# Last 512 tokens' end of a first layer spread over the turns of the second layer's attention; short rows of the last head pair put last

## The chip, the cores and the metric

The kernel runs on one core of one Trainium2 chip. The metric is device time in microseconds (us). Before the change it is 1535.13 us, the median of three runs (1533.04 to 1536.53). The profiled execution took 1535.0 us; its instructions span 1532.2 us of that, and 2.8 us lie around them.

## The reference

Input is one sequence `x` of 2048 tokens with 128 features, all in float32. Two layers of the same outer form run one after the other:

```
x  = L0_attn_x                                  # 1 x 2048 x 128
xn = layernorm(x)
s  = layernorm(xn + relu_attention(xn) @ w_out + b_out) * gamma + beta    # 16 heads of 8
g  = silu(routed_block(xn))       # 255 chosen tokens: attention, MLP; the others pass through
x  = x + s * g
xn = layernorm(x)
s  = softmax_attention(xn, causal)              # 16 heads of 64, output through W_O, + b_O
g  = silu(h @ w_down), h = silu(xn @ w_gate) * (xn @ w_up)                # hidden size 384
x  = x + s * g
```

The weights of the last feed-forward come as integers and are multiplied by 1/127.

## The kernel before

Tokens lie on the 128 partitions in 16 chunks of 128; four chunks make a block of 512 tokens, and `NQ` is 4 blocks. The order of the instructions on TensorE (PE), ScalarE (ACT) and VectorE (DVE) is the order in which the program calls them, since the whole body runs under a manual schedule; GpSimd (POOL) and the DMA queue of SyncE (SP) are ordered by the framework. [...]

**First layer.** `relu_attention` runs 256 steps (4 query blocks, 4 groups of 4 heads, 16 key chunks). Between the steps a generator `others` is advanced: the routed block, then `gated(qc)` for each query block. `gated` (lines 824 to 874) is the end of the layer for 512 tokens: sums are inverted and sent through DRAM to be widened (`wide<-inverse`, eight DMAs), `on` is multiplied by `wide` on POOL, multiplied by `w_out` on PE (L843), added to `xne` (L847), normalised, gated by `g0`, added to `xin`, normalised again, transposed (L100) and stored in `xn1T` (L191). Its `moments` (L882 to L889) take a square root on ACT (L198) and a Newton step on POOL (L203 to L206). For the first three blocks this is done between steps of the first attention. The last block's sums are only there once the last step has run, so `gated(3)` runs after it.

**Between the layers.** After the steps, `second.opened()` loads the second layer's weights, and `early` (line 1000) runs the feed-forward `ffn(i)` (L1018 to L1030) of blocks 0 to 2 and the first projections of head pair 0: keys 0 and 1, queries 0 and 1, values 0 and 1. `gated(3)` advances by one step after each piece of these. PSUM tiles here come from six one-bank buffers of the first layer. When `gated(3)` has ended, `ffn(3)` runs, and the attention begins.

**Second layer's attention.** `attention` works on 8 head pairs; a pair has 19 turns. A turn `r` holds two slots, each a score tile of two PSUM banks (there are two such tiles). The order of work in a turn is: scores of the turn (L1139), their maxima on DVE (mask L1156, maximum L1157), transposes of the previous turn's exponentials on PE (L1327) with their evictions, two on ACT and the rest on DVE (L1334), the exponentials of this turn on ACT (L1167), products with the values (`z`, L1182), and then what `other` hands out: one of the projections planned in `ahead`, or a step of the end of a finished query block (`divided` L1221/L1224, `output` L1234 to L1246). All PSUM tiles but scores and `z` come from a ring of three one-bank buffers with tag `t`. A score tile is free for the next turn when its exponentials are done.

The turns follow one list for every pair: rows 4 and 5, then 0 and 1, 6 and 7, 2 and 3, then the longer ones, up to rows 14 and 15 over the second half of the keys. Rows 0 to 3 need few keys, so their turns are short.

When the eighth pair's part of a query block is there, `output` adds it to `acc` (L1241), multiplies by the gate `g1` (L1244), adds `x1` (L1245) and stores 256 KB (L1246).

Of the kernel before, what the change touches and what calls it, by code (L numbers as in the profile page):

```python
# [11 lines left out]
F32 = mybir.dt.float32  # L12
F32R = mybir.dt.float32r
BF16 = mybir.dt.bfloat16
I32 = mybir.dt.int32
U32 = mybir.dt.uint32
AF = mybir.ActivationFunctionType
ALU = mybir.AluOpType
# [37 lines left out]
@with_exitstack  # L56
def mixed_layers_kernel(
    ctx: ExitStack,
    tc: tile.TileContext,
    a: dict,  # L60
    out: bass.AP,
):
    nc = tc.nc
    ctx.enter_context(nc.allow_non_contiguous_dma(reason="small weights and rows of sums"))

    const = ctx.enter_context(tc.tile_pool(name="const", bufs=1))
    small = ctx.enter_context(tc.tile_pool(name="small", bufs=4))


    ident = const.tile([P, P], F32, name="ident")  # L70
    make_identity(nc, ident)


    def row_load(name, n, pool):

        t = pool.tile([P, n], F32, name=f"row_{name}")
        nc.sync.dma_start(out=t, in_=a[name].partition_broadcast(P))
        return t


    xin = const.tile([P, NC, D], F32, name="xin")
    xn1T = const.tile([P, S], F32, name="xn1T")
    xsrc = a["x"].rearrange("(c p) d -> p c d", p=P)
    for i in range(NQ):
        nc.sync.dma_start(out=xin[:, 4 * i : 4 * i + 4, :], in_=xsrc[:, 4 * i : 4 * i + 4, :])


    with tc.manual_schedule(
        engines={mybir.EngineType.PE, mybir.EngineType.Activation, mybir.EngineType.DVE}
    ):  # L90
        second = layer1(ctx, tc, a, small, ident, xin, xn1T, row_load, out)
        layer0(ctx, tc, a, small, ident, xin, xn1T, row_load, second)
        second.attention()

# [10 lines left out]
def layer0(ctx, tc, a, small, ident, xin, xn1T, row_load, second):  # L105
    nc = tc.nc

    ends, steps, block = ExitStack(), ExitStack(), ExitStack()
    ps = ends.enter_context(tc.tile_pool(name="l0_ps", bufs=1, space=PSUM))
    dram = ctx.enter_context(tc.tile_pool(name="rb_dram", bufs=2, space=DRAM))  # L110
# [562 lines left out]
def relu_attention(  # L673
# [150 lines left out]
    def gated(qc):  # L824
# [13 lines left out]
        nc.gpsimd.tensor_tensor(on, on, wide, ALU.mult)  # L838
        yield
        yield  # L840
        t = bank([P, 4, D])
        for c4 in range(4):
            nc.tensor.matmul(  # L843
                t[:, c4, :], on[:, c4 * P : (c4 + 1) * P], w_out, start=True, stop=True
            )
        y = end.tile([P, 4, D], F32, tag="y", bufs=1, name="y")
        nc.vector.tensor_tensor(y, t, xne[:, cs, 0:D], ALU.add)  # L847
# [88 lines left out]
    steps.close()  # L936
    second.opened()
    ready.update(range(NQ))
    early = second.early(lambda: bank([P, 512], "s"))
    for _ in range(3):  # L940
        next(early)
    for _ in other:
        next(early, None)
    for _ in early:
        pass
    for _ in second.ffn(NQ - 1):
        pass
# [3 lines left out]
def layer1(ctx, tc, a, small, ident, x1, xn1T, row_load, out):  # L951


# [6 lines left out]
    def ffn_weights(pool, work):  # L960
# [6 lines left out]
        for _ in range(6):  # L967
            yield
        for wi, w in ffn_w.values():
            nc.vector.tensor_scalar(w, wi, 1.0 / 127.0, None, ALU.mult)  # L970
            work.add(d=0.8)
            yield

    def opened():

# [10 lines left out]
        nc.sync.dma_start(out=l1.W_O, in_=a["W_O"].rearrange("n p m -> p n m"))  # L986
        l1.b_o = row_load("b_O", D, lw)

        nc.gpsimd.tensor_scalar(W["W_Q"], W["W_Q"], 0.125, None, ALU.mult)
        nc.gpsimd.tensor_scalar(l1.b_q, l1.b_q, 0.125, None, ALU.mult)  # L990
        l1.g1 = lw.tile([P, NC, D], F32, name="g1")
        l1.acc = lw.tile([P, NC, D], F32, name="acc")

# [5 lines left out]
        )  # L999
        l1.wk = ctx.enter_context(tc.tile_pool(name="l1_w", bufs=2))  # L1000

    def early(bank):

        l1.bank, l1.turning = bank, False
        for i in range(NQ - 1):
            yield from ffn(i)
        for f, i in ((keys, 0), (queries, 0), (keys, 1), (queries, 1), (values, 0), (values, 1)):
            f(0, i)()
            yield


    def ffn(i):
        cols = slice(512 * i, 512 * i + 512)
        hT = l1.f.tile([P, NHB, 512], F32, tag="hT", bufs=2, name="hT")
        for hb in range(NHB):
            hs = slice(hb * P, (hb + 1) * P)
            gate, up = l1.bank(), l1.bank()
            nc.tensor.matmul(gate, ffn_w["w_gate"][1][:, hs], xn1T[:, cols], start=True, stop=True)  # L1018
            nc.tensor.matmul(up, ffn_w["w_up"][1][:, hs], xn1T[:, cols], start=True, stop=True)
            nc.scalar.activation(hT[:, hb, :], gate, AF.Silu)  # L1020
            nc.vector.tensor_tensor(hT[:, hb, :], hT[:, hb, :], up, ALU.mult)
            yield
        t = l1.bank().rearrange("p (c m) -> p c m", m=D)
        for c4 in range(4):
            for hb in range(NHB):
                nc.tensor.matmul(
                    t[:, c4, :], hT[:, hb, c4 * P : (c4 + 1) * P], ffn_w["w_down"][1][:, hb, :],
                    start=(hb == 0), stop=(hb == NHB - 1),
                )
        nc.scalar.activation(l1.g1[:, 4 * i : 4 * i + 4, :], t, AF.Silu)  # L1030
        yield
# [169 lines left out]
    def shares(pr, qc):  # L1201
# [11 lines left out]
        for h in range(n):  # L1213
            w = WIDE[pr, qc, h] = l1.wr.tile([P, 8, 64], F32, tag="wide", name="wide")
            nc.gpsimd.tensor_copy(w, s[:, h, :].unsqueeze(2).to_broadcast([P, 8, 64]))

    def divided(pr, qc, h):
        t = l1.bank().rearrange("p (a b) -> p a b", b=P)
# [4 lines left out]
        def later():  # L1223
            nc.vector.tensor_tensor(ZS[pr, qc, h], ZS[pr, qc, h], t, ALU.mult)  # L1224
            if h:
                nc.vector.tensor_tensor(ZS[pr, qc, 0], ZS[pr, qc, 0], ZS[pr, qc, 1], ALU.add)
# [3 lines left out]
    def output(pr, qc):  # L1230
# [7 lines left out]
        def later():  # L1238
            cs = slice(4 * qc, 4 * qc + 4)
            base = l1.b_o.unsqueeze(1).to_broadcast([P, 4, D]) if pr == 0 else l1.acc[:, cs, :]  # L1240
            nc.vector.tensor_tensor(l1.acc[:, cs, :], t, base, ALU.add)  # L1241
            if pr == NP - 1:
                res = l1.wr.tile([P, 4, D], F32, tag="res", bufs=1, name="res")
                nc.vector.tensor_tensor(res, l1.acc[:, cs, :], l1.g1[:, cs, :], ALU.mult)  # L1244
                nc.vector.tensor_tensor(res, res, x1[:, cs, :], ALU.add)  # L1245
                nc.sync.dma_start(out=out.rearrange("(c p) d -> p c d", p=P)[:, cs, :], in_=res)  # L1246

# [10 lines left out]

    order = []
    for c0, h in (  # L1260
        (4, 0), (0, 0), (6, 0), (2, 0), (8, 0), (8, 1), (10, 0), (10, 1), (12, 0), (14, 0),
        (12, 1), (14, 1),
    ):
        order += four(c0, h)
    per = len(order) // 2
    turns = [
        [[(pr, *row) for row in slot] for slot in order[i : i + 2]]
        for pr in range(NP) for i in range(0, 2 * per, 2)
    ]


    ahead = []
    for pr in range(NP):
        for turn, f, i in (
            (-7, queries, 1), (-6, keys, 0), (-5, keys, 1), (-3, queries, 0), (-2, values, 0),
            (-1, values, 1), (1, queries, 2), (3, keys, 2), (5, values, 2), (7, queries, 3),
            (9, keys, 3), (11, values, 3),
        ):
            ahead.append((pr * per + turn, f, (pr, i)))
    ahead.sort(key=lambda x: x[0])  # L1280
    ahead = ahead[6:]

# [53 lines left out]
    def kept(pr, c0, h, slot):  # L1336
# [6 lines left out]
        if not left[pr, qc]:  # L1343
# [5 lines left out]
            after.append((output, (pr, qc)))  # L1349

    def attention():
        nonlocal todo, n_slots, due, r, waited
        l1.ps = ctx.enter_context(tc.tile_pool(name="l1_ps", bufs=2, space=PSUM))
        l1.wr = ctx.enter_context(tc.tile_pool(name="l1_r", bufs=2, side="right"))
        l1.bank = lambda: l1.ps.tile([P, 4, P], F32, tag="t", bufs=3, name="m").rearrange(
            "p a b -> p (a b)"
        )
        l1.turning = True
        l1.z = l1.ps.tile([P, 2, 2, P], F32, tag="z", bufs=1, name="z")
        while r < len(turns) + 1 or todo or done or after:  # L1360
            slots = turns[r] if r < len(turns) else []
            old = sum(turns[r - 1], []) if 1 <= r < len(turns) + 1 else []
            while done:
                kept(*done.pop(0))
            new = []
            for rows in slots:
                maxima, what = scores(rows)
                maxima()
                new.append((rows, *what))
            evicted(turned(packed(old), [nc.scalar.copy, nc.scalar.copy, nc.vector.tensor_copy]))  # L1370
            for x in new:
                exponentials(*x)
            if after and after[0][0] in (ratios, shares):
                g, args = after.pop(0)
                g(*args)
                waited = r

            if todo:
# [13 lines left out]

            for few in (True, False):
                f = other(r, few)
                if f:
                    f()
            r += 1

    def other(r, small):

        nonlocal waited
        if ahead and ahead[0][0] <= r and not small:
            _, f, args = ahead.pop(0)
        elif after and waited < r and after[0][0] in (divided, output):
            f, args = after.pop(0)
# [63 lines left out]
```

## Time and profile before

| | |
|---|---|
| time, median of three runs | 1535.13 us (1533.04 to 1536.53) |
| profiled execution | 1535.0 us, span 1532.2 us |
| mean granted TensorE clock | 0.989 |
| DVE, ACT, POOL busy | 1109.7 us (72%), 961.6 us (63%), 307.9 us (20%) |
| first layer's attention ends on PE | 522.3 us |
| first score of the second attention | 578.6 us |
| last score of the second attention begins | 1506.9 us |
| last DVE instruction ends | 1528.7 us |
| one pair of heads in between | 117.5 us, of it PE busy 116.4 us |

The page gives busy time of each engine, then 40 slices of the span. A row of the timeline has the start, the time that the merged instructions cover, the engine and line, what is written from what, and in square brackets the idle time ahead of it with its releaser. A row of the chain of waits has the start, the length and what the end of the program waited for at that moment. A row of the table of stretches has the length of the stretch and, for each engine, busy time and number of instructions, then the granted clock. A float32 product on PE shows as two rows each; the fp32r scores and the transposes show as one.

### The profile page before, as it was taken

To read this page: it belongs to the slowest core of one execution; us is meant where nothing else is said; L and a number is where in the kernel's file an instruction comes from. 1 tells how busy PE (TensorE), PEld (TensorE's weight loads), DVE (VectorE), ACT (ScalarE), POOL (GpSimd) and SP (SyncE) were. 2 spreads that over 40 slices of the span, in tenths; PEclk is the share of its full clock that TensorE was granted. 3 is DMA by queue.
4 is the path that set the end of the run, shared out by engine and by line. 5 is a ranking of instruction groups with operands and counts; after the bars stand their busy time and mean duration, and the time that the engine had idled before them with its cause. 6 is when DMAs were issued, how large, how long until landed. Compare 5 with 4: busy or idle time off the path is not lost.

```text
span 1532.2 us, 27033 instructions
## 1 busy us (share of the span) xinstructions
PE 1462.9 (95%) x10374; PEld 886.6 (58%) x10374; DVE 1109.7 (72%) x1985; ACT 961.6 (63%) x2056; POOL 307.9 (20%) x409
## 2 busy tenths in 40 slices
PE   4999999999999968999999999999999999999997
PEld 2223333233222346777777777777777777777775
DVE  5798778877888646667667767767766767767775
ACT  2787778777888635556555655655655655655653
POOL 1000100024000001242242232232231242232210
PEclk9999999999999989999999999999999999999998
DMA  2000100000000210010001001001001001001000
GB/s 64 1 5 3 37 4 4 9 5 27 7 12 9 76 35 15 15 29 15 15 18 25 15 15 28 15 15 29 15 15 28 15 15 29 15 15 24 19 15 14
DMA packets 19681, 29.24 MB, mean 19 GB/s; under 512 B 5024, under 2 KB 13600, under 8 KB 19552
## 3 DMA queue, kind: packets, MB, share of 16 engines
q1 hardware_dynamic: 18864, 26.47, 7.4%
q8 instruction: 81, 1.33, 0.4%
q0 software_dynamic: 256, 0.79, 0.2%
q14 instruction: 48, 0.39, 0.1%
q10 hardware_dynamic: 432, 0.26, 0.1%
HBM read 7.69 MB, written 1.72 MB: 6 GB/s over the span
## 4 chain that ended last, share of the span: by engine, by line
PE 85%; DVE 7%; ACT 6%; issue 1%; DMA 0%; POOL 0%; ACTq 0%; DVEq 0%; POOLq 0%
PE t L1139 17%; PE z L1182 16%; PE t L1327 15%; PE t L801 13%; PE t L785 6%; PE m L1234 2%; PE m L1049 2%; PE m L1084 2%; PE t L695 2%; PE m L1221 2%; PE m L1099 2%; ACT rt L793 2%; ACT pt L1334 1%; DVE rt L795 1%; DVE junk L303 1%
## 5 line engine op out<-in xcount | busy, mean ns | idle before, releaser
L793 ACT ACTIVATE rt<-t 128x512 f32<-128x512 f32 x624 | 329.6, 608 | 73.4 <-PE t L785 72.5
L1157 DVE TENSOR_REDUCE tops<-t 128x1 f32<-128x1024 f32 (+4 forms) x320 | 334.7, 1063 | 53.4 <-PE t L1139 46.4
L1167 ACT ACTIVATE p<-t,tops 128x1024 f32<-128x1024 f32 (+7 forms) x384 | 330.6, 877 | 4.6 <-DVE tops L1157 4.6
L1139 PE MATMUL t<-k,q 128*128 128x512 f32 (+3 forms) x1280 | 319.0, 392 | 8.5 <-ACT p L1167 7.8
L1334 ACT COPY pt<-t 128x512 f32<-128x512 f32 (+2 forms) x320 | 149.2, 523 | 277.5 <-PE t L1327 277.5
L795 DVE TENSOR_SCALAR rt<-t 128x512 f32<-128x512 f32 x400 | 259.2, 684 | 36.7 <-PE t L785 31.9
L1327 PE MATMUL t<-ident,p 128*128 128x128 f32 x2176 | 278.0, 276 | 5.0
L801 PE MATMUL t<-rt,va 128*9 128x512 f32 x2048 | 268.2, 596 | 3.7 <-ACT part L817 3.7
L1182 PE MATMUL z<-pt,v 128*64 128x256 f32 (+1 forms) x2304 | 268.3, 374 | 0.5 <-ACT zs L1341 0.5
L1139 PEld LDWEIGHTS t<-k,q 128*128 128x128 f32 x1280 | 219.2, 189 | 81.3 <-issue 34.4
L1327 PEld LDWEIGHTS t<-ident,p 128*128 128x128 f32 x2176 | 244.4, 141 | 34.8 <-ACT pt L1334 17.2
L1182 PEld LDWEIGHTS z<-pt,v 128*64 128x64 f32 x2304 | 151.9, 136 | 87.3 <-issue 25.2
L1334 DVE COPY pt<-t 128x512 f32<-128x512 f32 (+2 forms) x320 | 180.5, 608 | 1.7 <-PE t L1327 1.7
L785 PEld LDWEIGHTS t<-qT,kT 32*128 32x128 f32 x1024 | 64.6, 181 | 185.2 <-ACT rt L793 112.1
L785 PE MATMUL t<-qT,kT 32*128 32x512 f32 x1024 | 156.9, 497 | 4.9 <-DVE rt L795 2.7
L1156 DVE TENSOR_TENSOR t<-t,mask_q 128x128 f32<-128x128 f32 (+1 forms) x192 | 65.1, 339 | 93.8 <-PE t L1139 85.0
L1072 POOL CAST q<-x 64x512 fp32r<-64x512 f32 x60 | 36.6, 610 | 409.1 <-ACT x L1070 407.3
L1167 ACT ACTIVATION_READ_ACCUMULATOR p<-t,tops 128x1 f32 x384 | 82.4, 215 | 0.0
L1224 DVE TENSOR_TENSOR zs<-zs,m 128x512 f32<-128x512 f32 x48 | 32.8, 688 | 67.1 <-PE m L1221 67.1
L1074 POOL TENSOR_TENSOR k<-x,k 64x512 fp32r<-64x512 f32 x60 | 76.2, 1271 | 4.6
L1074 POOL TENSOR_TENSOR q<-x,q 64x512 fp32r<-64x512 f32 x60 | 76.1, 1269 | 4.6
L1072 POOL CAST k<-x 64x512 fp32r<-64x512 f32 x60 | 36.5, 609 | 173.0 <-ACT x L1070 171.2
(244 smaller groups left out, 1097.1 us busy)
## 6 DMA issues: line engine op xcount, KB each, us to landing
q<-q SPq DMA_DIRECT2D x64, 256.0 KB
xin<-in_x SPq DMA_DIRECT2D x4, 256.0 KB
on<-part SPq DMA_DIRECT2D x64, 16.0 KB
wide<-inverse SPq DMA_DIRECT2D x32, 32.0 KB
out<-res SPq DMA_DIRECT2D x4, 256.0 KB
r_w<-in_w SPq DMA_DIRECT2D x2, 256.0 KB
mdram<-mrows SPq DMA_DIRECT2D x1, 512.0 KB
w_W_K<-in_W_K SPq DMA_DIRECT2D x1, 512.0 KB
```

The lines of the kernel that those rows point to most:

```text
L785: nc.tensor.matmul(t, kT[rows, g, kb * P : (kb + 1) * P], qTs[qc, g][rows, :], start=True, stop=True,)
L793: nc.scalar.activation(rt, t, AF.Relu, scale=scale)
L795: nc.vector.tensor_scalar(rt, t, scale, 0.0, ALU.mult, ALU.max)
L801: nc.tensor.matmul(acc[32 * j : 32 * j + HD0 + 1, :], va[:, kb, 4 * g + j, :], r[j], start=(kb == 0), stop=(kb == NC - 1),)
L1072: nc.gpsimd.tensor_copy(high, x[half(e), :])
L1074: nc.gpsimd.tensor_tensor(low, x[half(e), :], high, ALU.subtract)
L1139: nc.tensor.matmul(flat[:, lo + x : lo + y], q[:, part, c4 * P : (c4 + 1) * P], k[:, x:y], start=(part == 0), stop=(part == 1),)
L1157: nc.vector.tensor_reduce(M[pr, c // 4][:, h, c % 4, es], x, AX.X, ALU.max, negate=True)
L1167: nc.scalar.activation(p[:, lo : lo + n], flat[:, lo : lo + n], AF.Exp, bias=M[pr, c // 4][:, h, c % 4, e : e + 1], accum_out=Z[pr, c // 4 ...
L1182: nc.tensor.matmul(l1.z[half(e), slot, lo:2, :], V[pr, h][:, kb, half(e)], pts[e][:, kb, lo:2, :], start=(kb == 0), stop=(kb >= n0 - 1), s ...
L1327: nc.tensor.transpose(t[:, k + b, :], x[lo + b], ident)
L1334: copy(dst, t)
```

## The change

The end of the first layer for the last 512 tokens stops after its product with `w_out` and the addition to `xne`, which writes into `second.y`, the last four chunks of `acc`. The rest of it, and the whole feed-forward of that block, is cut into 12 pieces by `tail` that run at the ends of turns of pair 0. To keep what the pieces need, POOL copies the gate `g0` of that block and the three feed-forward weights. The square root becomes an integer estimate on DVE with four Newton steps on POOL.

The PSUM pool of the second layer opens right after the first layer's steps, so the feed-forwards of blocks 0 to 2 and the first projections also use its ring of three banks. Their order becomes: `ffn(0)`, then queries 1, keys 0 and keys 1 mixed with the parts of `ffn(1)`, the scores and maxima of turn 0, `ffn(2)` with queries 0 in it. Values 0 and 1 move into turn 0, queries 2 into turn 1. The gate of block 2 is kept raw, and its Silu is taken together with three other tiles in the piece of the third gate product.

In the last pair the rows 2, 3, 0 and 1 go to the end. `acc` is multiplied by the gate and added to `x1` on POOL after the seventh pair, so that the last `output` needs two DVE operations rather than three. The last query block is divided, added and stored in two halves. Once the turns are over, all of `ratios` and `shares`, and up to four steps of `other`, are taken in each round.

```diff
@@ relu_attention, gated
-        yield
-        yield
-        t = bank([P, 4, D])
+        for _ in range(2 if qc < NQ - 1 else 6):
+            yield
+        if qc < NQ - 1:
+            t = bank([P, 4, D])
+        else:
+            t = second.bank().rearrange("p (a b) -> p a b", b=D)
...
+        if qc == NQ - 1:
+            nc.vector.tensor_tensor(second.y, t, xne[:, cs, 0:D], ALU.add)
+            return
@@ relu_attention, after the steps
     steps.close()
-    second.opened()
+    second.opened(g0)
     ready.update(range(NQ))
-    early = second.early(lambda: bank([P, 512], "s"))
+    early = second.early()
     for _ in range(3):
         next(early)
     for _ in other:
-        next(early, None)
+        next(early)
     for _ in early:
         pass
-    for _ in second.ffn(NQ - 1):
-        pass
     ends.close()
@@ layer1, opened
+        end = slice(NC - 4, NC)
+        l1.y, l1.gate = l1.acc[:, end, :], l1.g1[:, end, :]
+        nc.gpsimd.tensor_copy(l1.gate, g0[:, end, :])
+        for n, (w,) in list(ffn_w.items()):
+            kept = lw.tile(list(w.shape), F32, name=f"f_{n}_last")
+            nc.gpsimd.tensor_copy(kept, w)
+            ffn_w[n] = w, kept
...
+        l1.ps = ctx.enter_context(tc.tile_pool(name="l1_ps", bufs=2, space=PSUM))
+        l1.bank = lambda: l1.ps.tile([P, 4, P], F32, tag="t", bufs=3, name="m").rearrange(
+            "p a b -> p (a b)"
+        )
+        l1.turns, l1.turning = attention(), False
@@ layer1, early
-        for i in range(NQ - 1):
-            yield from ffn(i)
-        for f, i in ((keys, 0), (queries, 0), (keys, 1), (queries, 1), (values, 0), (values, 1)):
+        yield from ffn(0)
+        hidden = ffn(1)
+        for f, i in ((queries, 1), (keys, 0), (keys, 1)):
             f(0, i)()
             yield
+            next(hidden)
+            yield
+        yield from hidden
+        next(l1.turns)
+        yield
+        hidden = ffn(NQ - 2)
+        next(hidden)
+        yield
+        queries(0, 0)()
+        yield
+        yield from hidden
@@ layer1, new
+    def moments(x):
...
+        for i in range(4):
+            nc.vector.bn_stats(st[:, i, :], x[:, i, :])
+            nc.vector.bn_aggr(mv[:, i, :], st[:, i, :])
+        nc.vector.tensor_scalar(v, mv[:, :, 1], 1e-5, None, ALU.add)
+        yi = y.bitcast(I32)
+        nc.vector.tensor_scalar(yi, v.bitcast(I32), 1, None, ALU.arith_shift_right)
+        nc.vector.tensor_scalar(yi, yi, -1.0, float(0x5F3759DF), ALU.mult, ALU.add)
+        for i in range(4):
+            nc.gpsimd.tensor_tensor(t, y, y, ALU.mult)
+            nc.gpsimd.tensor_tensor(t, t, v, ALU.mult)
+            nc.gpsimd.tensor_scalar(t, t, -0.5, 1.5, ALU.mult, ALU.add)
+            nc.gpsimd.tensor_tensor(r if i == 3 else y, y, t, ALU.mult)
+        return mv, r
+
+    def tail():
...
+        def first():
+            got.append(moments(y))
+        def gated():
+            mv, r = got.pop()
+            for c in range(4):
+                nc.vector.scalar_tensor_tensor(
+                    y[:, c, :], y[:, c, :], mv[:, c, 0:1], g[:, c, :], ALU.subtract, ALU.mult
+                )
+            for c in range(4):
+                nc.vector.scalar_tensor_tensor(
+                    x[:, c, :], y[:, c, :], r[:, c : c + 1], x[:, c, :], ALU.mult, ALU.add
+                )
+        def second():
+            got.append(moments(x))
+        def normal():
...
+        def turn():
+            t = l1.bank().rearrange("p (a b) -> p a b", b=P)
+            for c in range(4):
+                nc.tensor.transpose(t[:, c, :], y[:, c, :], ident)
+            return lambda: nc.scalar.copy(xn1T[:, cols], t.rearrange("p a b -> p (a b)"))
...
+        def raw(hb, t):
+            nc.scalar.copy(hs[hb], t)
+            if hb == NHB - 1:
+                for h in hs + [l1.g1[:, NC - 8 : NC - 4, :]]:
+                    nc.scalar.activation(h, h, AF.Silu)
+        def times(hb, t):
+            nc.vector.tensor_tensor(hs[hb], hs[hb], t, ALU.mult)
+        def down():
...
+            return lambda: nc.scalar.activation(g, t, AF.Silu)
+        out = [(f, (), False) for f in (first, gated, second, normal)] + [(turn, (), True)]
+        for n, later in (("w_gate", raw), ("w_up", times)):
+            out += [(hidden, (n, hb, later), True) for hb in range(NHB)]
+        return out + [(down, (), True)]
@@ layer1, output
+            if pr < NP - 1:
+                base = l1.b_o.unsqueeze(1).to_broadcast([P, 4, D]) if pr == 0 else acc
+                nc.vector.tensor_tensor(acc, t, base, ALU.add)
+                if pr == NP - 2:
+                    nc.gpsimd.tensor_tensor(acc, acc, g1, ALU.mult)
+                    nc.gpsimd.tensor_tensor(acc, acc, x1[:, cs, :], ALU.add)
+                return
...
+            for x in pieces(pr, qc):
+                nc.vector.tensor_tensor(res[:, x, :], t[:, x, :], g1[:, x, :], ALU.mult)
+                nc.vector.tensor_tensor(res[:, x, :], res[:, x, :], acc[:, x, :], ALU.add)
+                nc.sync.dma_start(out=dst[:, x, :], in_=res[:, x, :])
@@ layer1, the order of the turns
+        if pr == NP - 1:
+            order = [x for x in order if x not in ((0, 0), (2, 0))] + [(2, 0), (0, 0)]
...
+                (0, queries, 2), (2, keys, 2), (4, values, 2), (5, queries, 3), (7, keys, 3),
+                (9, values, 3), (11, queries, 0),
@@ layer1, attention, end of a turn
-            for few in (True, False):
-                f = other(r, few)
+            for few in (r > 2, False, True, True)[: 4 if ending else 2]:
+                f = other(r, few, ending)
+                if not f and few and pieces and pieces[0][2]:
+                    g, args, _ = pieces.pop(0)
+                    f = g(*args)
                 if f:
                     f()
+            if pieces and not pieces[0][2]:
+                g, args, _ = pieces.pop(0)
+                g(*args)
             r += 1
```

## The prediction

> **What bounds the kernel now.** I read the page first, then the granted clock and busy times in short stretches round the change of layers, then the timeline there and at the end, then the chain of waits.
>
> ```profile
> PE 1462.9 (95%) x10374; PEld 886.6 (58%) x10374; DVE 1109.7 (72%) x1985; ACT 961.6 (63%) x2056; POOL 307.9 (20%) x409
> ...
> PE 85%; DVE 7%; ACT 6%; issue 1%; DMA 0%; POOL 0%; ACTq 0%; DVEq 0%; POOLq 0%
> ```
>
> PE bounds the program as a whole: a pair of heads takes 117.5 us, 116.4 of them with PE busy. So the change can gain only where PE stands still, and PE work moved into the turns costs its full time. The table of stretches shows where it stands still:
>
> ```profile
> 552.00:556.00 4.00, 1.80 (x17) 1.61 (x15) 3.81 (x9) 3.91 (x7) 0.23 (x1) 1.00 0.17 37
> 556.00:560.00 4.00, 0.00 (x0) 0.00 (x0) 3.74 (x9) 0.62 (x1) 0.79 (x4) 0.62 0.70 175
> 560.00:564.00 4.00, 0.00 (x0) 0.00 (x0) 3.29 (x14) 0.16 (x1) 0.22 (x1) 0.50 0.15 50
> ...
> 580.00:582.00 2.00, 0.23 (x2) 0.03 (x1) 1.90 (x3) 1.12 (x1) 0.00 (x0) 1.00 0.00 0
> 582.00:584.00 2.00, 0.89 (x5) 0.68 (x5) 0.00 (x0) 1.93 (x5) 0.00 (x0) 1.00 0.00 0
> 584.00:586.00 2.00, 2.00 (x9) 1.80 (x9) 1.53 (x4) 0.00 (x0) 0.00 (x0) 0.56 0.00 0
> ```
>
> PE's busy time is the first figure after the length. DVE and ACT work through the end of the first layer while PE has nothing: 12.0 us idle in one piece. After it PE runs at half clock, and each of turns 0 to 2 waits again for maximum and exponential. From 540 to 600 PE is idle 18.5 us. The end is a chain of single steps:
>
> ```profile
> 1515.90 3.48 PE z L1182 x32
> ...
> 1520.97 0.62 POOL wide L1215
> ...
> 1522.34 1.30 DVE zs L1224 x2
> ...
> 1524.49 2.06 PE m L1234 x8
> ...
> 1528.03 0.69 DVE res L1245
> ```
>
> Last score 1506.91, last DVE end 1528.72, end 1532.2.
>
> **Up to turn 0: PE 523.1 to 559.6.** PE work, from the rows: three feed-forwards of six products at 0.86 and 24 half-products at 0.11 (7.8 each, 23.3), four projections at 0.86 (3.4), scores of turn 0 (1.66), `w_out` (0.9): 29.3. The start waits for the eviction of the old accumulator, on which the first product now depends (523.08 rather than 522.29). What is added in waits:
> - Queries 1 comes right after `ffn(0)`, about 531.7, but POOL ends scaling `w_W_Q` at 533.02 (its row starts 530.24, when the weights land). Wait 1.5. The four POOL copies ahead of it (0.61 and three of about 0.45) end before 530 and cost nothing.
> - Three banks in place of six. A projection holds its bank for two ACT rows (1.38) and the last of two DVE rows (0.75 each): about 2.5. Between it and the next use of that bank PE has 1.72 of work. Wait 0.8 for keys 0, keys 1, the `down` of `ffn(1)` and `w_out`, 3.2; bounds 0 (a bank free in time) and 1.2 each.
> - The last factor of each `down` waits for DVE: 0.4 to 0.9, about 2.1 for three.
>
> The sum is 36.2; with handovers I take 559.6. On SP the two DMAs of queries 1 now stand ahead of the eight `wide` loads. Those wait for `inverse` until 536.75 anyway, about when queries 1 is split; a delay of 1 us is covered, as `w_out`'s product stands at about 553 and `on` was ready at 544.7.
>
> **Turns 0 to 4: 559.6 to 586.4.** A turn's first score needs the exponential of the turn before, that needs the maximum, and the maximum stands on DVE behind the piece put at the end of the turn. Pieces on DVE: `first` and `second` 2.3 each (four pairs of 0.28 and 0.18 with gaps, three small ones), `gated` 2.3, `normal` 1.4. Each `moments` also puts 16 POOL steps of 0.28 ahead of the piece that follows: 4.5.
> - S1: raw copy, table load 1.28, exponential 1.0 after 559.6: 562.6.
> - S2: `values` added to 562.5, `first` to 564.8, maximum 1.15, exponential 1.0: 567.0.
> - S3: POOL to 569.4, `gated` to 570.6, short rows' maxima 2.1, four short exponentials 1.8: 574.6.
> - S4: maximum 574.1, evictions 1.0, `second` to 577.4, then PE's own work: 580.7.
> - S5: POOL to 582.0, `normal` 583.4, maximum 1.6, exponential 1.35: 586.4.
>
> Before, S5 is at 605.65, so 19.2 are won there. PE's own work in this stretch is about 20 of 26.8 us, so the pieces bound it, not PE. POOL's split of queries 2 comes 4 us later than it would; it is not needed until turn 5, where before had 18 us.
>
> Here **the clock rule** bears. The Trainium skill ("TensorE: Matmul & The Clock Gate", What's actually happening) gives half clock after about 3.4 us idle. The row is sharper: after the gap from 580.24 to 583.11, only 2.9 us, the clock is 0.56. By the rule one gap (before S3) would count, 1.7 us of half speed; by rows like those of 580 to 600 (mean 0.83) 20 us of work loses up to 4, half of it beside other waits. I take 1.5; bounds 0 and 3.5.
>
> **Left over for later turns.** Of `ffn(3)` the six products and `down` still run on PE: 5.2 + 2.6 = 7.8, full price. The transposes are in S5 already.
>
> **Silu among exponentials.** Two switches to Silu and back are put into turns 7 and 15. The trace:
>
> ```profile
> 552.34 1.38 ACT L1063 ACTIVATE k<-t,b_k 64x512 fp32r<-64x512 f32 x2
> ...
> 553.73 1.28 ACT L198 ACT_TABLE_LOAD   x1
> ...
> 555.02 0.21 ACT L198 ACTIVATE y<-ln_v 128x4 f32<-128x4 f32 x1
> ```
>
> The load starts when the row before ends, and the next starts when it ends: 1.28 in all. The skill ("ScalarE: Activation LUTs", What ACT_TABLE_LOAD costs) counts another 1.38 of drain per switch, and its Rules for kernel authors say to do all of one set before switching, which speaks against this change. In turn 7 ACT gets a copy 0.6, a load 1.28, four Silu 2.4, where its gap up to the next eviction is 2.05 (1494.86 to 1496.91): PE's fourth transposition bank comes 2.2 late. Then the load of Exp puts the exponentials 1.28 back, of which 0.7 shows. Turn 15: 0.5. Together 3.4 by the row, 8.9 by the rule (four drains more). I take 3.4; bounds 1 and 8.9. The loads taken out (Sqrt, Silu) lie in the stretch that is gone.
>
> Front: 19.2 − 1.5 − 7.8 − 3.4 = **6.5 won**.
>
> **The end.** Moving rows 0 to 3 takes the wait of turn 2 out of the last pair (before it PE waits 4.0 for DVE and ACT, with 1.2 of work in it: 2.8) and 0.7 of small evictions. After the last scores PE now has 15.7 of work (transposes 3.1, `z` 6.9, the rest 5.7) against 13.6, so those scores come 2.1 earlier too: 5.6 in all. But what follows is longer. From their start: maxima 5.0; evictions, two exponentials of 0.9 and four of 0.44 to 7.2; last bank 8.4; `z` of rows 14 and 15 waits behind that in PE's order, 11.9; its copy, the ratios, POOL 14.2, transposes and DVE 17.1, product 18.4, two DVE steps 19.9. The reciprocal of rows 0 to 3 stands behind these on DVE, so its chain runs on its own: 20.1, POOL 20.8, PE 21.4, DVE 22.2, product 23.4, last half 25.0, store 3.0 (before: 3.5 for 256 KB). That is 28.0 against 25.3: 2.7 lost. Net **2.9 won**; bounds −2.5 (the earlier scores not had) and +6 (the two chains overlap). The second store costs 0.4 of issue, inside the 3.0. POOL's eight steps of 1.27 in pair 6 lie beside POOL idle 73% of a pair; uncovered they would delay queries 2 by 2.5, four turns before it is due.
>
> **Sum** against the profiled execution: 1535.0 − 6.5 − 2.9 = 1525.6. The median of the runs, 1535.13, is the same within 0.02%. About 0.2% (3 us) is what a measurement of this kernel can tell from no change.
>
> **Rivals.**
> 1. *Pieces hide, PE bounds the first turns.* For: DVE was only 70% busy. If the pieces delay no maximum, S5 comes 7 earlier, Silu costs 1: 6.5 + 7 + 2.4 + 2.9 = 18.8, 1516. Against: the order on DVE puts each piece ahead of the next maximum. 0.20.
> 2. *Switches at the rule's price, or an end without gain.* 5.5 or 2.9 to 5.4 dearer: 1529 to 1531, taken as 1531. 0.20.
> 3. *Slower: the ring of three.* From turn 4 to 15 eight pieces each take a bank that ACT or DVE must empty before the transposes go on. The chain of waits has such a stop in before: 0.59 for an eviction with 0.45 of transposes behind it. If each piece costs one turn's stop plus an exponential (0.6 + 1.1 = 1.7), 13.6 are lost: 1539. From 1.2 per piece it eats the whole gain. Against: evictions of full banks in before mostly hide beside `z`. 0.09.
> 4. *It doesn't do what it says*: if waits up to S1 eat the lead (S5 near 596 rather than 586), 1535. 0.05.
>
> The forecast has 0.46, its own range 1520 to 1529.
>
> **Numbers.** Range 1513 to 1534: below, rival 1 with an end at +6; above, the bounds of Silu and of the end together. Faster 0.87, same 0.04, slower 0.09.
>
> **What would show it.** No idle PE over 5 us between 523 and 590; S1 at 562 to 563, S5 at 584 to 589; in turn 7 loads of 1.28 with an idle PE of 2 to 3; `w_W_Q` holding PE near 531.7; at the end a reciprocal on DVE behind the last but one result, and 27 to 29 us from the last scores to the end. It is wrong if pair 0 after turn 5 loses more than 4 beyond 7.8, or later pairs differ from 117.5.

## The result, and the profile after

The changed kernel takes 1529.55 us (median of six runs, 1529.15 to 1530.31), the kernel before 1535.93 in the same comparison (six runs, 1533.04 to 1536.9). The ratio is 0.9961, with a 95% interval of 0.9948 to 0.9974: faster, by 2.6 to 5.2 thousandths. The profiled execution took 1529.64 us with a span of 1527.5, against 1535.0 and 1532.2 before.

First the page of the changed kernel, its busy times and the shares of the chain of waits. Nothing in them answers the question of where the gain came from; PE is the bound as before, with the same number of instructions.

```profile
PE 1462.7 (96%) x10374; PEld 884.6 (58%) x10374; DVE 1110.9 (73%) x1988; ACT 965.7 (63%) x2060; POOL 324.5 (21%) x443
...
PE 84%; DVE 7%; ACT 6%; issue 2%; DMA 0%; POOL 0%; SPq 0%; ACTq 0%; POOLq 0%; DVEq 0%
```

The table of stretches of the changed kernel, over the same microseconds as before, shows it (columns as before: length, then busy time of PE, weight loads, DVE, ACT and POOL with the number of instructions, granted clock, DMA):

```profile
552.00:556.00 4.00, 3.58 (x15) 2.00 (x14) 2.79 (x4) 1.74 (x4) 0.00 (x0) 1.00 0.32 66
556.00:560.00 4.00, 3.59 (x29) 3.17 (x29) 0.69 (x1) 0.39 (x2) 0.00 (x0) 1.00 0.19 66
560.00:564.00 4.00, 2.91 (x20) 2.46 (x20) 2.92 (x11) 3.45 (x6) 0.00 (x0) 1.00 0.00 0
564.00:568.00 4.00, 3.86 (x26) 2.89 (x25) 3.86 (x11) 2.74 (x7) 2.44 (x13) 1.00 0.02 4
568.00:572.00 4.00, 2.34 (x15) 1.75 (x15) 3.82 (x7) 1.12 (x3) 3.54 (x8) 1.00 0.00 2
572.00:576.00 4.00, 0.00 (x0) 0.00 (x0) 3.86 (x7) 0.92 (x5) 0.84 (x1) 0.85 0.60 131
576.00:580.00 4.00, 3.15 (x8) 2.57 (x9) 3.72 (x16) 1.78 (x6) 0.32 (x2) 0.50 0.00 0
```

From 552 to 564, where PE was busy 1.8 of 12 us, it is now busy 10.1. But from 572 to 576 it has nothing at all, DVE is full, POOL is full in the row ahead, and half clock follows. The prediction reckoned with a pause before turn 3 (it put those scores at 574.6 and counted one gap there for the clock), but not with one of 6.4 us.

To see where the rest is, the span is cut at four moments that every version has: the first product of the feed-forward, the scores of turn 5, the first scores of pair 1, the last scores. Each figure is a difference of two start times on PE's timeline (the last one to the end of the span). Predicted are the prediction's own terms (64.8 is 586.4 - 523.1 plus 1.5 for the clock; 100.5 is 89.3 + 7.8 + 3.4).

| stretch, us | before | predicted | after |
|---|---|---|---|
| wait ahead of the first product | 0 | 0.8 | 0.8 |
| first product to turn 5 | 83.4 | 64.8 | 66.5 |
| turn 5 to pair 1 | 89.3 | 100.5 | 99.0 |
| pair 1 to the last scores | 811.9 | 806.3 | 809.6 |
| last scores to the end | 25.3 | 28.0 | 28.9 |

The front (the first three rows) won 6.35 us, with 6.5 predicted. The end (the last two) was to win 2.9 and **lost 1.3**. The sum is 5.1; the first layer ended 0.4 later in this execution, which makes the 4.7 of the span, and 0.7 less lay outside the span. So the gain was 5.4 us between the profiled executions and 6.4 between the medians, where 9.4 was predicted.

The end, in the chain of waits of the changed kernel (start, length, what the end waited for):

```profile
1498.71 2.05 PE t L1269 x12
...
1506.68 4.28 PE z L1312 x40
...
1512.48 0.62 POOL wide L1345
...
1515.16 0.70 DVE zs L1364
...
1516.00 1.14 PE m L1372 x8
...
1517.96 0.69 DVE res L1391
1518.65 0.12 DVE sums L1339
...
1519.59 0.67 PE m L1357 x4
...
1520.83 2.09 PE m L1372 x8
...
1524.19 0.42 DVE res L1391
```

The division of rows 12 to 15 (POOL at 1512.48, its factors on DVE to 1515.86), its product at 1516.00, then all of it again for rows 0 to 3, whose reciprocal (L1339) starts when the result of the others is ready. The last product takes 2.09 where the one at 1516.00 takes 1.14: PE had stood still for 2.46 us before the transposes of 1519.59 and for 0.58 after them, and its granted clock was 0.55 from 1520 to 1523.

### The profile page after: what moved, and what is told of

Same layout as the page of the kernel before. It is cut to its first block, busy times and chain, and to the rows that moved or that the text cites. A ratio compares the mean times of both kernels' runs of the same rounds, so it can differ in the third digit from the quotient of the medians.

```text
span 1527.5 us, 27075 instructions
## 1 busy us (share of the span) xinstructions
PE 1462.7 (96%) x10374; PEld 884.6 (58%) x10374; DVE 1110.9 (73%) x1988; ACT 965.7 (63%) x2060; POOL 324.5 (21%) x443
## 4 chain that ended last, share of the span: by engine, by line
PE 84%; DVE 7%; ACT 6%; issue 2%; DMA 0%; POOL 0%; SPq 0%; ACTq 0%; POOLq 0%; DVEq 0%
PE t L1269 17%; PE z L1312 16%; PE t L1481 14%; PE t L802 13%; PE t L786 6%; PE m L1372 2%; PE m L1179 2%; PE m L1214 2%; PE t L696 2%; PE m L1229 2%; PE m L1357 2%; ACT rt L794 2%; ACT pt L1488 1%; DVE rt L796 1%; DVE junk L304 1%
## 5 line engine op out<-in xcount | busy, mean ns | idle before, releaser
L1312 PEld LDWEIGHTS z<-pt,v 128*64 128x64 f32 x2304 | 151.8, 136 | 87.1 <-issue 24.9
L1362 DVE TENSOR_TENSOR zs<-zs,m 128x512 f32<-128x512 f32 (+1 forms) x49 | 32.8, 675 | 63.6 <-PE m L1357 63.4
L802 PEld LDWEIGHTS t<-rt,va 128*9 128x9 f32 x2048 | 30.7, 88 | 68.5 <-issue 60.0
```

Of the source, the lines that this page charges most:

```text
L802: nc.tensor.matmul(acc[32 * j : 32 * j + HD0 + 1, :], va[:, kb, 4 * g + j, :], r[j], start=(kb == 0), stop=(kb == NC - 1),)
L1312: nc.tensor.matmul(l1.z[half(e), slot, lo:2, :], V[pr, h][:, kb, half(e)], pts[e][:, kb, lo:2, :], start=(kb == 0), stop=(kb >= n0 - 1), s ...
```

## Experiments

The experiments are compared with runs of the kernel before on the same chip beside them; its medians there lay between 1535.2 and 1535.8. The table has the stretches as above. In runs with the same code, turn 5 to pair 1 agrees within 0.1, pair 1 to the last scores within 0.4, the last stretch within 0.6 (but for e9), so a microsecond is read more safely here, though from one profiled execution of each run, than from the times, whose intervals are 3 to 5 us wide. The first stretch is less steady: before and e3 have the same front and differ by 2.9, since half clock lasted longer in e3 (from 568 to 572 the granted clock was 0.68 in before and 0.50 in e3).

| run | time, us | ratio to before, 95% interval | product to turn 5 | turn 5 to pair 1 | pair 1 to last scores | last scores to end |
|---|---|---|---|---|---|---|
| changed kernel | 1529.55 | 0.9961 (0.9948 to 0.9974) | 66.5 | 99.05 | 809.6 | 28.9 |
| e1_old_order | 1526.00 | 0.9938 (0.9925 to 0.9952) | 66.2 | 99.05 | 811.8 | 24.5 |
| e2_front_only | 1527.92 | 0.9946 (0.9933 to 0.9960) | 66.5 | 99.03 | 811.9 | 25.5 |
| e3_end_only | 1537.29 | 1.0008 (0.9999 to 1.0016) | 86.3 | 89.35 | 809.4 | 29.3 |
| e4_queries2_early | 1529.07 | 0.9953 (0.9940 to 0.9967) | 68.3 | 99.02 | 809.6 | 29.3 |
| e5_early_shares | 1523.81 | 0.9924 (0.9911 to 0.9938) | 66.5 | 99.01 | 809.3 | 23.3 |
| e6_early_shares_old_order | 1524.15 | 0.9927 (0.9913 to 0.9941) | 66.5 | 99.02 | 811.9 | 21.4 |
| e7_no_silu | 1527.85 | 0.9950 (0.9936 to 0.9963) | 66.5 | 97.33 | 809.7 | 29.3 |
| e8_queries2_early_pool | 1527.84 | 0.9950 (0.9936 to 0.9964) | 64.9 | 99.02 | 809.7 | 29.4 |
| e9_both | 1522.67 | 0.9914 (0.9900 to 0.9928) | 64.9 | 99.04 | 809.6 | 24.9 |
| e10_no_pieces | 1522.49 | 0.9913 (0.9897 to 0.9928) | 59.5 | 99.02 | 809.7 | 28.9 |

### The two halves of the change apart: e2 and e3

e2 has the front of the changed kernel and the whole end of before; e3 the other way round. e2 against the changed kernel, cut to its core:

```diff
+            base = l1.b_o.unsqueeze(1).to_broadcast([P, 4, D]) if pr == 0 else l1.acc[:, cs, :]
+            nc.vector.tensor_tensor(l1.acc[:, cs, :], t, base, ALU.add)
+            if pr == NP - 1:
+                res = l1.wr.tile([P, 4, D], F32, tag="res", bufs=1, name="res")
...
-        if pr == NP - 1:
-            order = [x for x in order if x not in ((0, 0), (2, 0))] + [(2, 0), (0, 0)]
...
-        if pr == NP - 1:
-            plan = [
...
```

> The changed kernel with the whole end of before (order, three DVE steps, one store per block). My theory: the front alone wins 5.9 us, so 1529.6 beside 1535.5, and first scores of pair 1 come 5.9 earlier than before; that is the whole gain of the change, so no difference from the changed kernel beyond 1 us. Rival, the prediction's sum: 6.5 of 9.4 won, and the changed kernel 2.9 faster than this.

> Before with the new end alone (last pair's order, gate on POOL, halves, several steps a round). My theory: 1.0 to 1.3 us slower than before, the last scores 2.6 earlier and 28.9 us from them to the end. Rival, the prediction: 2.9 us faster than before.

The front alone takes 1527.92 us. In the stretches it is the changed kernel up to pair 1 and the kernel before after it. The end alone takes 1537.29, a ratio of 1.0008 (0.9999 to 1.0016): no gain, and on the stretches (809.4 + 29.3 against 811.9 + 25.3) 1.5 us slower. The rival, 2.9 us faster, is out. By the stretches the new end costs 1.0 us in the changed kernel and 1.5 in the kernel before; the times alone tell neither from nothing.

### The order of the last pair: e1

```diff
-        if (pr, qc) == (NP - 1, 0):
+        if (pr, qc) == (NP - 1, NQ - 1):
             return [slice(0, 2), slice(2, 4)]
...
-        if pr == NP - 1:
-            order = [x for x in order if x not in ((0, 0), (2, 0))] + [(2, 0), (0, 0)]
-        if pr == NP - 1:
-            plan = [
...
```

> The changed kernel with the last pair's turns and projections back in the order of the other pairs; the gate on POOL and the two halves of the last output stay (now for rows 12 to 15). My theory now: the new order brought the last scores only 2.6 us forward and made the stretch from them to the end 3.6 longer. So here the last scores come 2.6 later than in the changed kernel, and from them to the end it takes 25.3 - 0.7 (one DVE step fewer) - 0.5 (half a store) = 24.1 instead of 28.9: 2.2 us faster than the changed kernel, about 1527.4. Rival, the prediction's sum: last scores 5.6 later, so 0.8 slower than the changed kernel, about 1530.4.

The last scores come 2.25 later and the rest is 4.3 shorter: 2.1 won, as the theory said, and the time is 1526.00. So the other parts of the new end (one DVE step fewer, two halves) are good for 0.8 (837.2 from pair 1 to the end before, 836.4 here), where 1.2 was expected, and the order loses 2.1.

Why the last scores moved so little is seen in the kernel before. Its PE rows in the last pair, from the scores of turn 2 to those of turn 3:

```profile
1410.28 2.30 PE L1139 MATMUL t<-k,q 128*128 128x128 f32 x12
...
1412.41 1.71 PE L1327 MATMUL t<-ident,p 128*128 128x128 f32 x11
...
1414.05 1.30 PE L1182 MATMUL z<-pt,v 128*64 128x256 f32 x12
...
1415.82 2.08 PE L1139 MATMUL t<-k,q 128*128 128x512 f32 x8 [0.46 <-ACT p L1167]
```

The 4 us from 1411.8 to 1415.8, in which DVE and ACT make maxima and exponentials, hold 3.0 us of PE's own work, the transposes and the products with the values, and the last 0.6 of the scores ahead of them, not 1.2. PE waits 0.46, and 1.1 us in all between the first and the last scores of this pair (0.45 in the changed kernel). From the first scores of pair 1 to the last scores PE is busy 804.1 us before and 802.3 in the changed kernel: of the 2.3, 1.8 are PE work that moved behind the last scores, and about 0.6 are waits.

### The hole before turn 3: e4 and e8

DVE and POOL on the changed kernel's timeline, from the gated piece on, and the scores of turn 3:

```profile
567.61 1.21 DVE L1081 SCALAR_TENSOR_TENSOR acc<-acc,mv,g 128x128 f32<-128x128 f32 x4
...
568.90 1.27 POOL L1202 CAST q<-x 64x512 fp32r<-64x512 f32 x2
569.00 3.99 DVE L1085 SCALAR_TENSOR_TENSOR xin<-acc,inv,xin 128x128 f32<-128x128 f32 x4 [0.18 <-POOL inv L1062]
...
570.25 2.59 POOL L1204 TENSOR_TENSOR q<-x,q 64x512 fp32r<-64x512 f32 x2
...
576.85 3.57 PE L1269 MATMUL t<-k,q 128*128 128x512 f32 x8 [6.38 <-ACT p L1297]
```

Four steps of one shape take 1.21 at line 1081 and 3.99 at line 1085. Taken singly, the first of the slow ones runs 569.00 to 569.65 and the third 570.24 to 571.66. POOL splits queries 2 at that time: two casts of 0.61, then two subtractions of 1.27 (their length everywhere), the first of them from 570.25 to about 571.5. DVE's third step, which has two tensor inputs in SBUF like POOL's subtraction, ends 0.1 us after it.

e4 takes the split away from there: the projection of queries 2 goes ahead of the rest of `ffn(2)`, before the turns. e8 does the same but splits on POOL rather than on ACT and DVE. The edit of e8 (in e4 `queries(0, 2)()` stands in the place of the four lines):

```diff
         queries(0, 0)()
         yield
+        later = queries(0, 2)
+        l1.turning = True
+        later()
+        l1.turning = False
+        yield
...
-    ahead = ahead[4:]
+    ahead = [x for x in ahead[4:] if x[1:] != (queries, (0, 2))]
```

> The changed kernel with queries 2 of pair 0 projected before the down product of ffn(2) rather than in turn 1, so that POOL's split of it (1.27 for each half) no longer lies beside the gated piece on DVE. My theory: DVE's four steps at line 1085, which took 0.65 to 1.42 us each beside that split, fall to about 0.36 each like the four at line 1081 just before; that frees 2.6 us on DVE, and PE has one product (0.9) more ahead of turn 0's values. Scores of turn 3 come 1.5 earlier, the time is 1 to 1.7 us less than the changed kernel's. Rival: the steps are long by themselves (three operands in SBUF, or the half clock's stretch), they stay at 1.0 each and the time is 0.9 longer.

> As e4, but with the split of queries 2 done on POOL in the way of the later turns (one copy on ACT), while POOL is idle, so that its bank is held for 0.7 rather than 4 us. In e4 the gated piece's four steps fell to 0.35 each (2.7 us won on DVE) and 3.7 us were lost before turn 1, because ACT and DVE did that split and PE waited 1.38 and 0.47 for its bank. Theory: turn 1 comes only about 1.0 later than in the changed kernel, turn 3 1.7 earlier, the first scores of pair 1 1.5 earlier. Rival: the time won on DVE is taken up again by another wait before turn 5 and pair 1 comes no earlier.

In e4 the four steps fell to 0.35 each, so the mechanism holds. Its time did not: turn 1 came 4.2 later after the first product (43.4 instead of 39.2 us), because there ACT and DVE split queries 2 and PE waited 1.38 and 0.47 for the banks; then it ran at half clock (0.57 from 556 to 560, a gate product 1.91 instead of 1.02). 1.0 to 1.7 less was expected, and there is no difference. In e8 turn 1 is only 0.7 later, and the steps take this (its DVE timeline):

```profile
567.83 1.13 DVE L1086 SCALAR_TENSOR_TENSOR acc<-acc,mv,g 128x128 f32<-128x128 f32 x4
569.38 1.14 DVE L1090 SCALAR_TENSOR_TENSOR xin<-acc,inv,xin 128x128 f32<-128x128 f32 x4 [0.42 <-POOL inv L1067]
```

and turn 5 comes 1.6 earlier. The time is 1527.84, 1.7 less than the changed kernel, which the times alone could not tell from nothing. From these stretches I estimate that the contention cost turn 5 about 2.3 us: 1.6, and the 0.7 that moving the projection costs. A pause of 3.68 before turn 3 is left in e8, and half clock after it (0.50 from 576 to 580).

### What the pieces on DVE cost: e10

e10 leaves out the two norms, the gate and the addition to `x` for the last 512 tokens.

```diff
-        out = [(f, (), False) for f in (first, gated, second, normal)] + [(turn, (), True)]
+        out = 4 * [(lambda: None, (), False)] + [(turn, (), True)]
```

> The changed kernel with the four DVE pieces at the ends of turns 0 to 3 (the two norms, the gate and the addition to x for the last 512 tokens) left out, with nothing in their place; the pieces on PE stay where they are. It prices what those four pieces cost the first turns. Prediction: DVE bounds turns 0 to 4 and the pieces cost about 7 us there, plus the 2.6 that the split on POOL adds; then the fifth turn's scores come 57 to 59.5 us after the first feed-forward product, instead of 66.5. Rival 1 of the prediction (the pieces hide beside PE's work): they come at 63 to 66, the 2.6 of the split at most.

Turn 5 comes at 59.5, 7.0 earlier, at the edge of what the prediction's reading expects and far from the rival. The stretches of e10 lack the hole, and with it the half clock:

```profile
568.00:572.00 4.00, 2.21 (x15) 1.61 (x14) 3.78 (x7) 2.61 (x12) 3.61 (x4) 1.00 0.04 8
572.00:576.00 4.00, 3.83 (x23) 2.98 (x25) 3.02 (x6) 2.38 (x7) 0.13 (x1) 1.00 0.57 125
576.00:580.00 4.00, 4.00 (x24) 2.63 (x23) 1.82 (x5) 2.34 (x5) 0.75 (x2) 1.00 0.00 0
```

If the two add up, about 2.3 of the 7.0 are the split on POOL (the estimate from e8) and 4.7 the pieces with the half clock that they bring; how much of the 4.7 is the clock, no run shows. The pieces do bound the first turns.

### Silu among the exponentials: e7

ACT and PE in turn 7 of the changed kernel:

```profile
610.01 1.28 ACT L1117 ACT_TABLE_LOAD   x1
...
611.30 1.15 ACT L1117 ACTIVATE acc<-acc 128x512 f32<-128x512 f32 x2
...
614.12 1.18 PE L1481 MATMUL t<-ident,p 128*128 128x128 f32 x6 [1.17 <-ACT x L1200]
...
615.32 1.28 ACT L1297 ACT_TABLE_LOAD   x1
...
616.62 1.11 ACT L1297 ACTIVATE p<-t,tops 128x1024 f32<-128x1024 f32 x1
```

Each load is followed by its activation 1.29 to 1.30 after its start, so there is no drain on top; PE waits 1.17.

```diff
-                    nc.scalar.activation(h, h, AF.Silu)
+                    nc.scalar.copy(h, h)
...
-            return lambda: nc.scalar.activation(g, t, AF.Silu)
+            return lambda: nc.scalar.copy(g, t)
```

> The changed kernel with the Silu of the last blocks' feed-forward (the four tiles in turn 7 and the gate in turn 15) left out, copies in their place, so that no table is loaded among the exponentials. My theory, from the trace: PE stood 1.2 us for it in turn 7 and nothing in turn 15, so the stretch from turn 5 to the first scores of pair 1 gets 1.2 to 1.5 shorter (97.6 instead of 99.05). The prediction's price was 3.4 (95.6), the price with the drain that the Trainium skill counts 8.9 (90.1).

The stretch is 97.33, so the switches cost 1.7 us, all of them in turn 7: half of the prediction's 3.4, a little over my later 1.2 to 1.5, and a fifth of the 8.9 estimated by the rule of the Trainium skill ("ScalarE: Activation LUTs", What ACT_TABLE_LOAD costs).

### Dividing before the end: e5, e6 and e9

The sum of the exponentials is known when the last exponential is done; the program asked for the reciprocal only after the products with the values. In e5 `ratios` and `shares` of the last pair's end blocks are called right after their exponentials, and their factors are transposed behind `z`. The edit does one thing more: what `other` hands out once the turns are over (`f`, the DVE steps behind the output products) is held back in `held` until the last product has been asked for. e6 is that on e1. e9 is e5 with e8.

```diff
+    def shared(slots):
+        for pr, c, h, e in sum(slots, []):
+            if pr == NP - 1 and c // 4 in final:
+                rows_of[c // 4] -= 1
+                if not rows_of[c // 4]:
+                    if halves(c // 4) == 2:
+                        ratios(pr, c // 4)
+                    shares(pr, c // 4)
...
             for x in new:
                 exponentials(*x)
+            shared(slots)
...
+                        if not keys_of[c // 4]:
+                            todo += [(widened, (pr, c // 4, i)) for i in range(halves(c // 4))]
                     todo.append((lambda *x: done.append(x), (pr, c // 2 * 2, h, slot)))
...
-                if f:
+                if f and ending:
+                    held.append(f)
+                elif f:
                     f()
```

> The changed kernel, with the new order; the reciprocals of the last pair's first and last query blocks (ratios, shares, the widening on POOL) are issued as soon as their exponentials are, not after their z products, and the widened factors are transposed on PE right behind z. My theory: the new order loses at the end because two divisions run one after the other behind z, 28.9 us from the last scores to the end; with the divisions ahead of z the second block's chain lies beside the first's: the last DVE step comes 6.4 earlier, so 22.5 from the last scores to the end and about 6 us less than the changed kernel, near 1523. Rival: the end is bound by z and the small exponentials (PE in order), not by the divisions; then it gains under 2.

> The same early divisions on the run with the old order of the last pair (e1), for rows 12 to 15. One division instead of two was behind z there, so it gains less: z's end to the multiplication was about 3.0, now 1.2, so 1.8 less than e1, 22.7 from the last scores to the end. If e5 is faster than this by 1 to 3 us, the new order is worth its 2.6 only with early divisions; if this is faster, the new order is not worth it in either form.

> e5 (early divisions, new order) and e8 (queries 2 early, split on POOL) together. The two lie in stretches that don't touch, so their gains should add: 1.6 in the front (first scores of pair 1 163.9 us after the first feed-forward product instead of 165.5) and 5.5 at the end (23.3 instead of 28.9 from the last scores to the end, with pair 1 to the last scores at 809.3): about 1522.3, 7 less than the changed kernel and 13 less than before. Rival: the earlier start is eaten somewhere between, and it stays at e5's 1523.8.

The end of e5 on its timeline:

```profile
1505.33 0.20 DVE L1339 RECIPROCAL sums<-sums 128x8 f32<-128x8 f32 x1 [0.86 <-ACT p L1297]
...
1512.43 0.69 DVE L1362 TENSOR_TENSOR zs<-zs,m 128x512 f32<-128x512 f32 x1 [1.18 <-ACT zs L1495]
...
1514.39 1.95 PE L1372 MATMUL m<-w_W_O,zs 128*128 128x128 f32 x16
...
1518.13 0.43 DVE L1391 TENSOR_TENSOR res<-res,acc 128x256 f32<-128x256 f32 x1
```

The reciprocal of rows 0 to 3 is at 1505.33 instead of 1518.57, and both output products run as one row of 16. The last scores are 23.3 from the end, 5.6 less (6.4 expected), and the time is 1523.81. I estimate that about 0.9 of the 5.6 is the clock: 16 output products take 1.95 here, where the last 8 of the changed kernel took 2.09 alone. What of the rest is due to the early reciprocals and what to holding back the last DVE steps, no run separates. From pair 1 to the end the four forms take, by the stretches:

| | division behind z | division ahead of z |
|---|---|---|
| rows 12 to 15 last | 836.4 (e1) | 833.3 (e6) |
| rows 0 to 3 last | 838.5 (changed kernel) | 832.6 (e5) |

So the new order turns from a loss of 2.1 into a gain of 0.7 once the divisions lie ahead. The 0.7 is below what the times can tell (1523.81 and 1524.15), and the 1 to 3 us expected were not seen; that part stays open. e6 also won more than the 1.8 expected: 3.1. Most of the excess is clock again: its widening and output products behind `z` take 1.09 and 1.49, those of e1 1.67 and 2.05.

e9 takes 1522.67 us, a ratio of 0.9914 (0.9900 to 0.9928) to before, faster than both kernels. It is 1.1 less than e5, where 1.5 was expected; its front has the 1.6. In its profiled execution the last `z` (32 products) took 5.15 instead of 3.46 in e5, with a granted clock of 0.61 from 1504 to 1508, so the end shows 24.9 there.

## Why the prediction came out as it did

The direction was right and the mechanism of the front was right, but 1525.6 was 4 us too low, and nearly all of it is one step: **the end**. The 1529.55 lies just above the 1520 to 1529 that I gave my own forecast, and in the 1529 to 1531 of the second rival.

- **"Moving rows 0 to 3 takes the wait of turn 2 out of the last pair … 2.8 … and 0.7 of small evictions"** is the step that failed. The last scores came 2.3 earlier, not 5.6. I counted a stretch in which the chain of waits lay on DVE and ACT as idle time of PE; PE's own rows show 0.46 of waiting there. Of the 5.6 only the 2.1 of moved work is nearly confirmed (1.8); waits gave 0.6.
- **The tail**: 28.0 predicted, 28.9 measured. Step by step it fits (last bank 8.4 and 8.0, reciprocal of rows 0 to 3 done at 20.1 and 20.1 after the last scores); the last product took 2.09 rather than 1.14, at half clock, and that is the 0.9. I had allowed 1.2 for it, though the row of before that I showed has 2.06 for the same product. Net −1.3 in place of +2.9, inside the bounds given (−2.5), whose lower one was "the earlier scores not had".
- **Up to turn 0**: 559.6 predicted, 559.61 in the trace. That it fits so closely is luck: PE waited 4.2 us rather than 6.8 (`w_W_Q` 1.19 for 1.5, the banks about 1.25 for 3.2, the factors of `down` 1.76 for 2.1), and its own work took 31.9 rather than 29.3. The terms as written also add to 36.1, not 36.2.
- **Turns 0 to 4**: turn 1 562.6 and 562.65, turn 2 567.0 and 566.58, as reckoned; turn 3 2.3 late, turn 5 3.6 late (1.5 of it priced as clock). What was missing is the split of queries 2 on POOL beside the gated piece: I priced its delay as harmless because nobody needs queries 2 until turn 5, and did not ask whom it slows. Two of the named showings failed here: no idle PE over 5 us (6.4), and turn 5 at 584 to 589 (590.0).
- **Left over**: 7.8 and 8.0 (97.33 in e7 less 89.34). So the ring of three, rival 3, cost nothing that shows: eight more tiles went through it at the price of their PE work.
- **Silu**: 3.4 and 1.7. The load by the row of 1.28 was right; the second return to Exp and turn 15 show no wait. PE stood 1.17 in turn 7, where 2 to 3 was named.
- The two misses of the front, +1.7 at turn 5 and −1.7 at Silu, cancel. 6.35 against 6.5 is therefore right as a sum by luck, and less right as a list.

Of the rivals, the second had half the truth: an end without gain, without dear switches.

## What to carry to other kernels

A stretch of the chain that lies on DVE and ACT isn't idle time of PE: before it is booked as a gain, sum PE's own rows inside it. When work is put behind the last scores, look at what is asked for behind it: here each division waited for products that it does not need, and asking earlier, with the last DVE steps held back, was worth 5.6 us where reordering lost 2.1. And when a piece goes onto DVE, look at what POOL does at that moment, not only at who waits for POOL.

## What the runs showed of the hardware

DVE steps with two tensor inputs in SBUF took 0.65 us beside POOL's casts and up to 1.42 beside POOL's subtractions, 0.35 without either (e4 and e8), while POOL's subtractions kept their 1.27. The Trainium skill says this ("SBUF — State Buffer", Who interferes with whom: a DVE instruction with two SBUF inputs contends with a GpSimd instruction that reads SBUF, and the order of issue decides who waits); the ends of DVE's steps 0.1 us after POOL's agree. That DVE was the one to wait is seen, the order is not: the third step and the first subtraction start 0.01 apart. I had not weighed that rule. Halving of the clock followed shorter pauses than I reckoned with: the last product of the changed kernel took 2.09 instead of 1.14 after a pause of 2.46, 0.66 of work and a pause of 0.58, and in e4 a gate product took 1.91 instead of 1.02 after pauses of 1.38 and 0.47 with 1.1 of work between. With the same code in a stretch, half clock also comes and lasts differently from one execution to another: the front of before took 83.4 us, that of e3 86.3, and the last `z` 3.46 in e5 and 5.15 in e9.
